# Two layers in one program: other dates, lanes and queues for the side work of the first two sequences

## The chip, the cores and the metric

The kernel runs on one core of a Trainium2 chip. The metric is the device time of one execution in microseconds. Before the change the median of three runs is 4860.24 us (4858.21 to 4866.17). All data are float32.

## The reference

Eight sequences of 1024 tokens with 256 features go through two layers. Cut to what matters:

```python
xn = layernorm(x)
x = x + causal_attention(xn) + routed_experts(xn)   # layer 0, 16 heads of 16
xn = layernorm(x)
x = x + attention(xn) + butterfly_ffn(xn)           # layer 1, 16 heads of 16
```

- `causal_attention` takes its softmax over the keys of a masked score matrix (masked entries are -10000, not minus infinity), so that the sum of later values enters with a small weight.
- `routed_experts` takes the softmax of 8 router logits, the best expert of each token, that expert's 256 x 256 matrix and bias, and multiplies by the gate.
- Layer 1's `attention` works on a log-mapped input `v`, its queries multiplied by a learned metric (two tanh layers); its output is multiplied by 0.1 and clipped.
- `butterfly_ffn` is a 256 to 1024 projection, ten butterfly stages, GELU, ten stages and a 1024 to 256 projection. The butterflies are linear, so they can be folded into the projections once for all tokens.

## The kernel before, in words

**Order.** Sixteen attentions follow one another: a0, a1, b0, a2, b1, a3 and so on (a is layer 0, b layer 1, the number the sequence). Each has four groups of heads, each group two halves of 512 queries, each half a number of *steps*, one for 128 keys: 4 and 8 for the causal layer, 8 and 8 for the other. So a0 is steps 1 to 48 and a1 steps 49 to 96. In a step TensorE computes the scores of two pairs of heads (L478), ScalarE takes the exponential (L485), for a block on the diagonal POOL clears what lies beyond it (`affine_select`, L487), and TensorE weighs the values (L503) one step later. Beside it runs a first pass for a later group: scores (L435), a mask added by VectorE where needed (L440) and row maxima (L444). The diagonal blocks of a0 are the four steps of each first half and the last four of each second half.

**Warm-up.** The first group's maxima have no scores to run beside. They are taken ahead of step 1 in twelve rounds of two maxima (the loop with `fill.step = -100`), with the step number at -99 to -88.

**Side work.** Everything else is written as generators, put as tasks into six lanes of a planner, `Fill`. A task has a cost (the TensorE time that it is thought to take, in ns; FULL is 855), a date `due`, a first step `after`, and a lead; its rank is `due - lead`. Only the head of a lane can run. After each step `spend` gives the tasks a budget, which follows from what is still to be done by each date (`rate`), and takes the ready task of lowest rank. A generator that yields `Rest` or `Later` cannot run again until so many steps have passed; tasks that last yielded `Rest` are moreover advanced, one piece every half step and at no cost, by `idle_engines`. `finish_due` runs all that is due at the start of a step to its end, one piece after another. The engines' queues are in order and the program's order is what this planner writes; each engine then waits on semaphores only.

**The tasks of the first sequence.** `gates0` computes values and router logits (per 128 tokens two matmuls and two VectorE additions, L614, L581, L619) and the best expert. `later0` makes suffix sums of the values: per tile one or two matmuls, and the running sum `rest` on POOL (L732, L734). `route0` ranks the tokens by expert (L657 to L698), scatters the normalized tokens into `sorted_d` in device memory with eight indirect DMAs issued by POOL (L703), two to a half step, and adds a bias to x on POOL (L570). `experts` handles 15 tiles of sorted tokens, each with a gather of the expert's matrix by POOL (L783), a load of the tokens by SP (L782), transposes (L806) and matmuls (L798), and a store to `mixed_d` by SP (L812). `collect` gathers the results (L829). `finish0` waits until a sequence is collected (`mixed`), transposes the attention's output (`outputs`) and projects it.

**The fold.** `multiply_paths` multiplies seven arrays of 128 x 2048, one after another, on POOL (L869). `fold` applies the products to the projections (`within`, L879, on TensorE), scales between blocks (`across`: ScalarE L893, VectorE L902 and L905, a copy by POOL L908), transposes (L947) and stores the folded weights. Layer 1 cannot begin without them.

The dates are set in `begin_attention` (L1209 on), where `s` holds the first steps of the four groups and the end: for a0 `s` is 0, 12, 24, 36, 48, and `starts[8]` is 96.

Of the kernel before, what the change touches and what calls it, by code (L numbers as in the profile page):

```python
# [12 lines left out]
ALU = mybir.AluOpType  # L13
# [9 lines left out]
DH = 1024  # L23
# [29 lines left out]


class Task:
    def __init__(self, gen, cost, due, after=0, lead=0):
        self.gen, self.cost, self.due, self.ready = gen, cost, due, after
        self.light = True
        self.rank = due - lead
# [142 lines left out]
def two_layers(ctx: ExitStack, tc: tile.TileContext, a: dict, out: bass.AP):  # L202
# [82 lines left out]
    paths = []  # L285
# [355 lines left out]
    def route0(att):  # L641

        b, n = att.b, att.n
        while b not in gates_of:
            yield Rest(0.5)
        yield Later(1)
        hot, gate = gates_of[b]
        shape = [P, NT, NE]

        rank = small.tile(shape, F32, tag="rank", name=f"rank_{n}", bufs=1)
        tot = small.tile(shape, F32, tag="tot", name=f"tot_{n}", bufs=1)
        of_e = small.tile([P, 3, NE], F32, tag="of_e", name=f"of_e_{n}", bufs=1)
# [12 lines left out]
        square = [P, NE, NE]  # L667
        sq = work.tile(square, F32, tag="es", name=f"sq_{n}", bufs=1)
        DVE.tensor_tensor(
            sq, tot[:, 0].unsqueeze(2).to_broadcast(square),  # L670
            tiles_from.unsqueeze(1).to_broadcast(square), ALU.is_gt,
        )
        DVE.tensor_reduce(num, sq, AX.X, ALU.add)
        DVE.tensor_tensor(sq, upto, num.unsqueeze(1).to_broadcast(square), ALU.mult)
        DVE.tensor_reduce(end, sq, AX.X, ALU.add)
        DVE.tensor_tensor(base, end, num, ALU.subtract)
        yield Rest(0.5)
        DVE.scalar_tensor_tensor(
            rank, base.unsqueeze(1).to_broadcast(shape), float(P), rank, ALU.mult, ALU.add
        )  # L680
        DVE.tensor_tensor(rank, rank, hot, ALU.mult)
        top = small.tile([P, NT], F32, tag="top", name=f"pos_{n}")
        DVE.tensor_reduce(top, rank, AX.X, ALU.add)
        slot_of = small.tile([P, NT], U32, tag="slot", name=f"slot_{n}")
        DVE.tensor_copy(slot_of, top)
        yield Rest(0.5)

        shape = [P, NS, NE]
        wide = work.tile(shape, F32, tag="es", name=f"wide_{n}", bufs=1)
        DVE.tensor_tensor(  # L690
            wide, end.unsqueeze(1).to_broadcast(shape), slot_no.unsqueeze(2).to_broadcast(shape),
            ALU.is_le,
        )
        ex = small.tile([P, NS], F32, tag="ex", name=f"ex_{n}", bufs=1)
        DVE.tensor_reduce(ex, wide, AX.X, ALU.add)
        DVE.tensor_scalar(ex, ex, float(NE - 1), float(P), ALU.min, ALU.mult)
        rows = small.tile([P, NS], U32, tag="rows", name=f"rows_{n}")
        DVE.tensor_scalar(rows, ex, row, None, ALU.add)  # L698
        yield Rest(0.5)
        xn, held = xn0.pop(b)  # L700
        yield from in_sorted.take()
        for t in range(NT):
            POOL.indirect_dma_start(  # L703
                sorted_d[:, :], bass.IndirectOffsetOnAxis(ap=slot_of[:, t : t + 1], axis=0),
                xn[:, t, :], None,
            )
            if t % 2:
                yield Rest(0.5)
        first.free(held)
        route_of[b] = slot_of, rows, gate  # L710
        yield from add_to_all(xs[b], outb)

    def later0(att):

        n = att.n
        while att.b not in gates_of:
            yield Rest(0.5)
        slot = None
        if att.b:
            slot = yield from second.take()  # L720
            later = work.tile([P, NT, D], F32, tag="second", name=f"later_{n}", bufs=1)
        else:
            later = work.tile([P, NT, D], F32, tag="h", name=f"later_{n}")
        att.slot = slot
        yield Later(0)
        rest = new = None
        for t in range(NT - 1, -1, -1):
            own = att.vals[:, t, :, 0:3:2, :]
            if t:
                new = small.tile([P, 8, 2, 16], F32, tag="rest", name=f"rest_{n}_{t}")  # L730
                if rest is None:
                    POOL.tensor_copy(new, own)  # L732
                else:
                    POOL.tensor_tensor(new, rest, own, ALU.add)  # L734
            ps = bank(f"later_{n}_{t}")
            PE.matmul(ps[:, :D], tri, own, start=True, stop=(rest is None))
            if rest is not None:
                PE.matmul(ps[:, :D], ones, rest, start=False, stop=True)
            ACT.copy(later[:, t, :], ps[:, :D])
            rest = new  # L740
            yield FULL
        att.later = later
# [98 lines left out]
    def finish0(att):  # L841
        b, n = att.b, att.n
        x = xs[b]
        while b not in mixed:
            yield Rest(0.5)
        sums = new_stats(f"b{b}")
        yield Later(0)
        for h in range(2):
            yield from att.outputs(h)
            for i in range(4):  # L850
                t = 4 * h + i
                ps = bank(f"y_{n}_{t}")
# [12 lines left out]

    def multiply_paths():

        for t in paths[1:]:
            POOL.tensor_tensor(paths[0], paths[0], t, ALU.mult)  # L869
            yield Rest(1)  # L870
        POOL.tensor_tensor(conb, conb, downb, ALU.add)
        folded.append("paths")

# [335 lines left out]
    def begin_attention(i):  # L1209
# [14 lines left out]
        if layer == 0 and b == 0:  # L1224
# [1 line left out]
            fill.add(0, later0(at[0, 0]), 8 * FULL, s[0] + 4)  # L1226
            fill.add(1, route0(at[0, 0]), 1, s[1])
            fill.add(1, prepare0(at[0, 1]), 4 * FULL, s[3])
            fill.add(1, gates0(at[0, 1]), 8 * FULL, s[4])
            fill.add(1, route0(at[0, 1]), 1, s[4])  # L1230
            fill.add(1, later0(at[0, 1]), 8 * FULL, s[4])
            fill.add(2, experts(0), 20 * FULL, s[4] - 8, 0, 24)
            fill.add(2, collect(0), 0, s[4])
            fill.add(2, experts(1), 20 * FULL, starts[8] - 10, 0, 24)
            fill.add(2, collect(1), 0, starts[8])
            fill.add(3, multiply_paths(), 0, s[1])
            fill.add(3, fold(), 12 * FULL, s[4] - 4)
        elif layer == 0 and b == 1:
            fill.add(0, prepare1(at[1, 0]), 8 * FULL, s[3])
            fill.add(0, values1(at[1, 0]), 8 * FULL, s[4])  # L1240
# [5 lines left out]
        else:  # L1246
            if b == 0:
                fill.add(1, prepare0(at[0, 2]), 4 * FULL, s[2], s[0] + 2)
            if b + 1 < NB:
                fill.add(0, prepare1(at[1, b + 1]), 8 * FULL, s[3], 0, 24)  # L1250
                fill.add(3, metric1(at[1, b + 1]), 32 * FULL, s[4] + 8 if b + 2 < NB else s[3])
            if b + 2 < NB:
                fill.add(1, gates0(at[0, b + 2]), 8 * FULL, s[1] + 4, s[0] + 2, 12)
                fill.add(1, route0(at[0, b + 2]), 1, s[2], 0, 20)
                fill.add(1, later0(at[0, b + 2]), 8 * FULL, s[4])
                fill.add(2, experts(b + 2), 20 * FULL, s[4] + 16, 0, 48)
                fill.add(4, collect(b + 2), 0, s[4] + 42)
            if b == NB - 2:
                fill.add(0, values1(at[1, b + 1]), 8 * FULL, s[4])
# [70 lines left out]
    while halves[0].i == 0:  # L1330
        first_pass(1)
        first_pass(0)
        fill.step += 1
        fill.now = fill.step
        fill.idle_engines()
        fill.spend(2 * FULL, 0.0)
        fill.release()
        put(now)
        now += 1
# [174 lines left out]
```

## Time and profile before

| | |
|---|---|
| median of three runs | 4860.24 us |
| the profiled execution | 4863.26 us |
| its span, first to last instruction | 4861.3 us |
| busy: PE / DVE / ACT / POOL | 4682.4 / 3070.2 / 2219.5 / 773.4 us |
| mean granted TensorE clock | 0.982 |
| DMA | 158.27 MB, 33 GB/s on average |

The page lists the busy time of each engine, the same in 40 slices of 121.5 us each (a digit is the busy share in tenths), and the costliest groups of instructions by line. A line of the form `L734 POOL TENSOR_TENSOR ...` is line 734 of the kernel; `x48` counts instructions. In the list of waits, `PE av_a L503 <- POOL p_a L487: 12.1, 1, 12.1` says that TensorE's matmul of line 503 waited for POOL's line 487, in total 12.1 us, once, the longest wait 12.1 us. The same questions can be put to a stretch of the span, given in us from its start. Names lose their numbers: `a0` and `a1` both show as `a`. PE is the matmul stream, PEld its weight loads.

### The profile page before, as it was taken

The page shows a single profiled execution, that of the slowest core. Times are in us where ns is not written, and L with a number is a line of the kernel's source. Part 1 is how long each engine was busy: PE and PEld are TensorE (multiplying, and loading weights), DVE is VectorE, ACT ScalarE, POOL GpSimd, SP SyncE. Part 2 cuts the span into 40 slices and gives each one's busy share as a digit, 9 for nine tenths or more (in the row PEclk, how much of TensorE's full clock was granted, in tenths as well). Part 3 has the DMA queues.
Part 4 walks back from the last instruction along what each step waited for, and adds up shares of the span by engine and source line. Part 5 has one row for each costly group of instructions (what it writes and reads, how often), then busy time and mean ns, then how long its engine had stood idle before and what let it go on. Part 6 is the DMA issues. An engine that isn't in the chain of part 4 may idle for free.

```text
span 4861.3 us, 69082 instructions
## 1 busy us (share of the span) xinstructions
PE 4682.4 (96%) x27808; PEld 1876.4 (39%) x27808; DVE 3070.2 (63%) x5010; ACT 2219.5 (46%) x2925; POOL 773.4 (16%) x1308
## 2 busy tenths in 40 slices
PE   7879999999999999999999999999999999999998
PEld 3334344344333443334443344334443344333332
DVE  5666665665666657666576666766667665666553
ACT  1343444544455444554345544455444544455544
POOL 3333300211120111201102111021211111110000
PEclk7989999999999999999999999999999999999999
DMA  3111200111001110012000110011100110000000
GB/s 136 61 59 59 71 2 16 33 54 40 12 18 33 55 36 3 23 39 68 15 1 28 40 62 15 1 39 40 54 13 10 34 55 27 20 1 10 1 9 9
DMA packets 85679, 158.27 MB, mean 33 GB/s; under 512 B 12657, under 2 KB 67569, under 8 KB 82161
## 3 DMA queue, kind: packets, MB, share of 16 engines
q1 hardware_dynamic: 69616, 89.88, 5.5%
q0 software_dynamic: 15744, 63.98, 4.0%
q8 instruction: 220, 3.60, 0.3%
q14 instruction: 99, 0.80, 0.1%
HBM read 117.25 MB, written 36.57 MB: 32 GB/s over the span
## 4 chain that ended last, share of the span: by engine, by line
PE 86%; DVE 6%; ACT 3%; issue 3%; POOL 1%; DMA 1%; POOLq 0%; DVEq 0%; SPq 0%; ACTq 0%
PE sc_b L478 18%; PE av_b L503 10%; PE sc_a L478 10%; PE mx_b L435 6%; PE av_a L503 5%; PE w L1149 5%; PE mx_a L435 5%; PE f L390 5%; PE h_b L390 3%; PE g_b L1076 2%; PE e L798 2%; ACT p_b L485 1%; PE q_b L390 1%; PE v_b L1036 1%; PE k_b L390 1%
## 5 line engine op out<-in xcount | busy, mean ns | idle before, releaser
L444 DVE TENSOR_REDUCE mm_b<-mx_b 128x2 f32<-128x1024 f32 x1024 | 1251.8, 1223 | 754.2 <-PE mx_b L435 753.5
L485 ACT ACTIVATE p_b<-sc_b 128x1024 f32<-128x1024 f32 x1024 | 1044.9, 1023 | 1092.2 <-PE mx_b L435 630.9
L435 PE MATMUL mx_b<-kT_b,qT_b 32*128 32x512 f32 x4096 | 1158.3, 642 | 10.9 <-ACT p_b L485 7.0
L478 PE MATMUL sc_b<-qT_b,kT_b 32*128 32x512 f32 x4096 | 1141.2, 638 | 7.9 <-ACT p_b L485 2.7
L485 ACT ACTIVATE p_a<-sc_a 128x1024 f32<-128x1024 f32 (+3 forms) x768 | 620.2, 809 | 905.2 <-PE sc_a L478 636.5
L444 DVE TENSOR_REDUCE mm_a<-mx_a 128x2 f32<-128x1024 f32 (+3 forms) x768 | 734.3, 957 | 219.7 <-PE mx_a L435 201.2
L435 PE MATMUL mx_a<-kT_a,qT_a 32*128 32x512 f32 (+3 forms) x3072 | 715.9, 549 | 15.4 <-DVE mm_a L444 6.6
L478 PE MATMUL sc_a<-qT_a,kT_a 32*128 32x512 f32 (+3 forms) x3072 | 713.3, 542 | 3.3 <-DVE mm_a L444 2.0
L503 PE MATMUL av_b<-p_b,vals 128*32 128x512 f32 x4096 | 554.1, 605 | 1.5 <-ACT p_b L485 1.5
L478 PEld LDWEIGHTS sc_b<-qT_b,kT_b 32*128 32x128 f32 x4096 | 305.9, 183 | 622.3 <-issue 402.1
L440 DVE TENSOR_TENSOR mx_a<-mx_a,cst 128x256 f32<-128x256 f32 x512 | 220.0, 430 | 389.4 <-PE sc_a L478 184.0
L487 POOL TENSOR_SCALAR_AFFINE_SELECT p_a<-p_a 128x256 f32<-128x256 f32 x512 | 209.6, 410 | 1355.7 <-ACT p_a L485 1337.2
L478 PEld LDWEIGHTS sc_a<-qT_a,kT_a 32*128 32x128 f32 x3072 | 234.5, 186 | 378.4 <-issue 273.0
L503 PE MATMUL av_a<-p_a,vals 128*32 128x512 f32 (+3 forms) x3072 | 337.6, 506 | 13.0 <-POOL p_a L487 13.0
L435 PEld LDWEIGHTS mx_b<-kT_b,qT_b 32*128 32x128 f32 x4096 | 307.1, 183 | 56.0 <-ACT p_b L485 42.2
L783 POOL DMA_INDIRECT ew<-in_ew,rows_a x120 | 116.6, 972 | 1081.9 <-PE mx_b L435 439.9
L1149 PE MATMUL w<-wcon,f 128*128 128x256 f32 x1024 | 276.5, 399 | 0.0
L435 PEld LDWEIGHTS mx_a<-kT_a,qT_a 32*128 32x128 f32 x3072 | 238.0, 188 | 70.5 <-ACT p_a L485 34.7
L1149 PEld LDWEIGHTS w<-wcon,f 128*128 128x128 f32 x1024 | 179.6, 191 | 141.7 <-issue 119.2
L503 PEld LDWEIGHTS av_b<-p_b,vals 128*32 128x32 f32 x4096 | 81.7, 108 | 391.5 <-issue 382.6
L390 PE MATMUL f<-xT_b,wexp 128*128 128x512 f32 x512 | 223.9, 595 | 0.0
L503 PEld LDWEIGHTS av_a<-p_a,vals 128*32 128x32 f32 x3072 | 62.3, 109 | 277.6 <-issue 208.7
(211 smaller groups left out, 4214.9 us busy)
## 6 DMA issues: line engine op xcount, KB each, us to landing
ew<-sorted_d SPq DMA_DIRECT2D x120, 128.0 KB, 3.1
mixed_d<-ew SPq DMA_DIRECT2D x120, 128.0 KB, 1.7
x<-in_x SPq DMA_DIRECT2D x8, 1024.0 KB, 5.6
wexp<-wexp_d SPq DMA_DIRECT2D x8, 1024.0 KB, 6.5
wcon<-wcon_d SPq DMA_DIRECT2D x8, 1024.0 KB, 6.3
out<-x SPq DMA_DIRECT2D x8, 1024.0 KB, 9.2
paths<-in_paths SPq DMA_DIRECT2D x7, 1024.0 KB, 12.5
w<-in_w1t SPq DMA_DIRECT2D x8, 512.0 KB, 3.8
```

Source lines behind the costliest of these rows:

```text
L390: PE.matmul(ps, w[:, c, cols : cols + P], rhs[:, c, h * 512 : (h + 1) * 512], start=(c == 0), stop=(c == 1),)
L435: PE.matmul(sc[:, j, :w], qT[r : r + 32, t * P : (t + 1) * P], kT[r : r + 32, k * 512 : k * 512 + w], start=True, stop=True,)
L440: DVE.tensor_tensor(sc[:, :, w - P : w], sc[:, :, w - P : w], negmask.unsqueeze(1).to_broadcast([P, 2, P]), ALU.add,)
L444: DVE.tensor_reduce(mm[:, t, 2 * pr : 2 * pr + 2, k], sc[:, :, :w], AX.X, ALU.max)
L478: PE.matmul(sc[:, j, c0:], kT[r : r + 32, kt * P : (kt + 1) * P], qT[r : r + 32, h * 512 + c0 : (h + 1) * 512], start=True, stop=True,)
L485: ACT.activation(p[:, :, c0:], sc[:, :, c0:], AF.Exp, scale=0.25)
L487: POOL.affine_select(p[:, :, c0 : c0 + P], p[:, :, c0 : c0 + P], [[0, 2], [1, P]], ALU.is_ge, 0.0, base=0, channel_multiplier=-1,)
L503: PE.matmul(av[32 * i : 32 * i + 32, c0:], self.vals[:, kt, 4 * (g // 2) + i, odd : odd + 2, :].rearrange("p e d -> p (e d)"), p2[i // 2][ ...
L783: POOL.indirect_dma_start(halves[:, s % 2, : 3 * D], None, a["ew"], bass.IndirectOffsetOnAxis(ap=rows[:, s : s + 1], axis=0),)
L798: PE.matmul(ps[:, :D], was[:, c * P : (c + 1) * P], w[:, c * D : (c + 1) * D], start=(c == 0), stop=(c == 1),)
L1076: PE.matmul(ps, w2t[:, m, c * P : (c + 1) * P], hT[:, m, :], start=(m == 0), stop=(m == 3),)
L1149: PE.matmul(ps[:, :D], hT[k // 4][:, k % 4, i * P : (i + 1) * P], wcon[:, k, :], start=(k == 0), stop=(k == 7),)
```

## The change

- A task's default `after` is minus infinity, not 0, so tasks without a date of their own are ready in the warm-up. Those that had 0 written out now have `s[0]`, or `s[0] - 99` for `experts(0)` and `fold`.
- In each round of the warm-up the idle engines are served twice, at the round's number and half a step later.
- `multiply_paths` multiplies halves of 1024 columns and rests half a step after each.
- `route0` rests half a step after each scatter, not after every second one.
- `later0` keeps its running sum on VectorE for sequence 0 (`on`), on POOL for the others.
- `finish0` runs `outputs` of a half before it waits for `mixed`.
- Dates, leads and lanes of sequences 0 and 1 differ, as below. `later0` of a1 moves from lane 1 to lane 0.

```diff
-    def __init__(self, gen, cost, due, after=0, lead=0):
+    def __init__(self, gen, cost, due, after=-math.inf, lead=0):
...
                 xn[:, t, :], None,
             )
-            if t % 2:
-                yield Rest(0.5)
+            yield Rest(0.5)
...
+                on = POOL if att.b else DVE
                 if rest is None:
-                    POOL.tensor_copy(new, own)
+                    on.tensor_copy(new, own)
                 else:
-                    POOL.tensor_tensor(new, rest, own, ALU.add)
+                    on.tensor_tensor(new, rest, own, ALU.add)
...
         x = xs[b]
-        while b not in mixed:
-            yield Rest(0.5)
         sums = new_stats(f"b{b}")
         yield Later(0)
         for h in range(2):
             yield from att.outputs(h)
+            while b not in mixed:
+                yield Later(0.5)
...
         for t in paths[1:]:
-            POOL.tensor_tensor(paths[0], paths[0], t, ALU.mult)
-            yield Rest(1)
+            for i in range(2):
+                part = slice(i * DH, (i + 1) * DH)
+                POOL.tensor_tensor(paths[0][:, part], paths[0][:, part], t[:, part], ALU.mult)
+                yield Rest(0.5)
...
             fill.add(1, prepare0(at[0, 1]), 4 * FULL, s[3])
-            fill.add(1, gates0(at[0, 1]), 8 * FULL, s[4])
-            fill.add(1, route0(at[0, 1]), 1, s[4])
-            fill.add(1, later0(at[0, 1]), 8 * FULL, s[4])
-            fill.add(2, experts(0), 20 * FULL, s[4] - 8, 0, 24)
-            fill.add(2, collect(0), 0, s[4])
-            fill.add(2, experts(1), 20 * FULL, starts[8] - 10, 0, 24)
+            fill.add(1, gates0(at[0, 1]), 8 * FULL, s[4], s[0], 40)
+            fill.add(1, route0(at[0, 1]), 1, s[4], s[0], 40)
+            fill.add(0, later0(at[0, 1]), 8 * FULL, s[4])
+            fill.add(2, experts(0), 20 * FULL, s[4] - 4, s[0] - 99, 44)
+            fill.add(2, collect(0), 0, s[4] + 4)
+            fill.add(2, experts(1), 20 * FULL, starts[8] - 10, s[0], 24)
             fill.add(2, collect(1), 0, starts[8])
             fill.add(3, multiply_paths(), 0, s[1])
-            fill.add(3, fold(), 12 * FULL, s[4] - 4)
+            fill.add(3, fold(), 12 * FULL, s[4] + 4, s[0] - 99, 30)
...
         fill.step += 1
-        fill.now = fill.step
-        fill.idle_engines()
+        for fill.now in (fill.step, fill.step + 0.5):
+            fill.idle_engines()
         fill.spend(2 * FULL, 0.0)
```

For the later sequences three tasks (`prepare1`, `route0`, `experts`) have `s[0]` in place of 0 as their first step.

More of the change, by code (lines that the diff above doesn't have):

```diff
@@ L1249, in begin_attention @@
             if b + 1 < NB:
-                fill.add(0, prepare1(at[1, b + 1]), 8 * FULL, s[3], 0, 24)
+                fill.add(0, prepare1(at[1, b + 1]), 8 * FULL, s[3], s[0], 24)
                 fill.add(3, metric1(at[1, b + 1]), 32 * FULL, s[4] + 8 if b + 2 < NB else s[3])
@@ L1253, in begin_attention @@
                 fill.add(1, gates0(at[0, b + 2]), 8 * FULL, s[1] + 4, s[0] + 2, 12)
-                fill.add(1, route0(at[0, b + 2]), 1, s[2], 0, 20)
+                fill.add(1, route0(at[0, b + 2]), 1, s[2], s[0], 20)
                 fill.add(1, later0(at[0, b + 2]), 8 * FULL, s[4])
-                fill.add(2, experts(b + 2), 20 * FULL, s[4] + 16, 0, 48)
+                fill.add(2, experts(b + 2), 20 * FULL, s[4] + 16, s[0], 48)
                 fill.add(4, collect(b + 2), 0, s[4] + 42)
```

## The prediction

> **What bounds the kernel now.** First the page, busy shares and slices:
>
> ```profile
> PE 4682.4 (96%) x27808; PEld 1876.4 (39%) x27808; DVE 3070.2 (63%) x5010; ACT 2219.5 (46%) x2925; POOL 773.4 (16%) x1308
> ...
> PE   7879999999999999999999999999999999999998
> ...
> POOL 3333300211120111201102111021211111110000
> PEclk7989999999999999999999999999999999999999
> ```
>
> TensorE fills the span; its 179 us of idleness lie almost wholly in the first three slices, where POOL is busiest and the granted clock below full. So I cut the start into stages and asked for the busy time of each. Cuts: first maximum matmul (25.2), first value matmul of a0 (57.4), first score matmul (67.9), and the score matmuls after that, eight records to a step: steps 1 to 12 end at 169.0, 13 to 36 at 287.9, 37 to 48 (the end of a0) at 395.0. Columns: window, its length, busy time of PE, PEld, DVE, ACT, POOL, clock, DMA share, GB/s.
>
> ```profile
> 25.20:57.40 32.20, 26.91 (x101) 11.59 (x101) 29.90 (x48) 2.06 (x4) 0.00 (x0) 0.56 0.64 214
> 57.40:67.90 10.50, 10.48 (x36) 8.44 (x36) 4.34 (x16) 0.00 (x1) 0.00 (x0) 0.72 0.00 0
> 67.90:169.00 101.10, 68.81 (x356) 26.93 (x355) 49.51 (x99) 24.83 (x39) 59.88 (x67) 0.75 0.13 44
> 169.00:287.90 118.90, 115.25 (x755) 52.23 (x751) 89.86 (x189) 56.30 (x91) 30.59 (x64) 0.99 0.18 61
> 287.90:395.00 107.10, 73.36 (x390) 32.09 (x390) 60.35 (x130) 39.84 (x71) 45.86 (x82) 0.79 0.20 68
> ```
>
> Steps 13 to 36 show what this stretch can do: PE idle 3.6 of 118.9 us, full clock. The two stages of twelve steps beside it lose 32 and 34 us to idleness and more to the halved clock; in the warm-up (first row) VectorE is full (29.9 of 32.2) and POOL does nothing. What ended the idle time, 67.9 to 395, in the waits of PE:
>
> ```profile
> PE wx L947 <- POOL wx L908: 19.4, 4, 17.1
> PE av_a L503 <- POOL p_a L487: 12.1, 1, 12.1
> PE later_a L738 <- POOL rest_a L734: 7.4, 3, 3.6
> PE later_a L738 <- POOL rest_a L732: 5.8, 2, 4.0
> PE e L806 <- DMA ew<-sorted_d: 4.5, 1, 4.5
> ```
>
> All are chains through POOL or a transfer. The groups of POOL and DVE in steps 1 to 12 say which:
>
> ```profile
> L869 POOL TENSOR_TENSOR paths<-paths,paths 128x2048 f32<-128x2048 f32 x6 | 27.0, 4508 | 0.0
> L703 POOL DMA_INDIRECT sorted_d<-xn_a,slot_a x8 | 8.0, 995 | 14.7 <-DMA sorted_d<-xn_a,slot_a 13.3 <-DVE slot_a L685 1.4
> ...
> L669 DVE TENSOR_TENSOR sq_a<-tot_a,cst 128x64 f32<-128x64 f32 x1 | 3.7, 3715 | 0.0
> L551 DVE TENSOR_TENSOR on_a<-es_a,rc_a 128x256 f32<-128x256 f32 x1 | 3.6, 3560 | 0.0
> ```
>
> Six path products of 4.5 us stand in POOL's queue ahead of masks (L487) and suffix sums (L734); eight scatters hold it for 22.7 us, as each waits for the one before to land; and L669 and L551, some 0.23 and 0.42 us elsewhere, end with a product.
>
> **The change, part by part.** The sum is made against the profiled execution: 4863.3 us (span 4861.3 and 2.0 around it), 3.0 over the median.
>
> What a step costs. Fill in steps 13 to 36 by spacing in the chain: 11 expert tiles at 1.06 with 11 transposes at 0.38 (15.8), 8 value tiles at 0.99 (7.9), four projections at 1.96 (7.8), 16 transposes (2.0), four path matmul groups at 1.06 (4.2), the bias (1.7): 39.4. (118.9 - 39.4) / 24 = 3.3 us a step, twelve steps 40.
>
> *Warm-up, 32.2 us.* Now no task is ready before step 0, for the default date is 0 and the warm-up counts from -99; value tiles run alone afterwards (10.5 us). With the new default twelve rounds offer 1.7 us of fill each. By the ranks: rounds 1 to 4 the eight value tiles, 5 and 6 the gate's small operations, 7 to 10 the eight suffix-sum tiles, 11 and 12 the ranks' matmuls and the first four path groups. VectorE pays: 8 x (0.425 + 0.156) = 4.6, ten small operations at 0.2 (2.1), seven suffix sums moved from POOL to DVE at 0.42 (L551's usual duration; 3.0), routing's 11 at 0.2 (2.3): 12. The path products start on an idle POOL as soon as the paths have landed (their 8 KB packets arrive from 20.3 to 41.1 us) and take 27 us, until about 52. Until then a DVE operation with two SBUF inputs can wait for a half product, 4.5 / 2: the gate's four and two sums, six of them, 0 to 13.5 us; I take half a wait each, 6. VectorE's 2.3 us of idleness fill up. 32.2 + 12 + 6 - 2.3 = 48, so step 1 starts near 73; bounds 67 (no collision) and 90 (TensorE kept at half clock: 26.9 and twice the 19 us of added matmuls, 65). The polls in half steps and conb's add (0.74) lie on the idle POOL; the two weight loads of the fold go past SP, which has nothing else by then.
>
> The row for collisions is L669. [...] The clock row reads 0.56 with PE busy 26.9 of 32.2. [...]
>
> *Steps 1 to 12, 101.1 us.* Gone: products, suffix sums, path groups. Left: 40, the bias 1.7 and three expert tiles (3.3). Routing's first scatter moves from step 8 to step 1, two a step to step 5, each 2.7 us of POOL (they start at 135.16, 137.85, 140.51) with two masks at 0.41: 6.2 us a step. Queued behind them are the masks of steps 1 to 4, all diagonal; the weighing of every step waits for those. 4 x (6.2 - 3.3) = 11.6; bounds 0 (the weighing lags a step) and 22.7. The fold's scaling moves here from steps 23 on: per step two ACT (0.50), two DVE (0.48) and a POOL copy (0.40) that waits for DVE, at 2.4 us a time in the old place (28.9 / 12), where PE was hardly idle; nothing, or 10 if masks queue behind it. I take 4 with the clock. Sum 61.
>
> *Steps 13 to 36, 118.9.* Experts come first (rank 0), one tile every second step because of the waits between them; path groups and transposes share the others, so value tiles of a1 come later, five rather than eight. Three fewer, 3.0, and nothing else: 115 (bounds 110, 125). On SP the store of the first folded weight now stands among the experts' loads; it waits for one ScalarE copy (L883, 0.59), and a tile has two steps until it is needed: 0 to 1.
>
> *Steps 37 to 48, 107.1.* Gone is what is forced at its date: three expert tiles at step 40 (the 4.5 us wait) and the fold at 44 (19.4). Fill: projections 7.8, two expert tiles 2.9, three value tiles 3.0, transposes 3.4, suffix sums 6.4, ranks 0.5: 24. With 40: 64. By the ranks a1's gates end near step 43 and its scatters start near 47, so up to seven are forced at 48: 7 x 2.7 and eight adds at 0.73, 25 us of POOL ahead of a mask, less the 7 us a weighing can lag. Bounds 0 (scatters done by then) and 25; I take 12, between a paced and a forced row. Small waits 5. Sum 81.
>
> *After.* Turning outputs ahead of the wait costs nothing: the transposes (two groups of 0.5) run beside the last gather. But collect(0) now ends at 52, not 48, so finish0's projections come three steps later: 0 to 15, taken 5, for prepare1 starts later while rates go by dates. For sequences 2 to 7 mixed is set long before, and dates of s[0] for 0 change nothing. Single scatters there are spread; 0, at most 5 either way.
>
> End of step 48: 73 + 61 + 115 + 81 = 330 for 395, gain 65, less 5: 60. 4863.3 - 60 = 4803, in a median execution 4800. From 600 on PE is busy for 4182.6 of 4261 us at full clock, so that all of it moves forward unchanged.
>
> **Rivals.**
> 1. The warm-up becomes the bound: half clock, step 1 at 90, and the diagonal scatters cost 22.7, not 11.6. 28 less: 4828. For it: the clock 0.56; against: PE busy is mostly VectorE's back-pressure.
> 2. The forced stretch only moves: step 48 takes the full 25, and the waits of 37 to 48 stay otherwise (107). 26 less: 4826. For it: serial routing cannot be shortened; against: the fold, 19.4, has no date there.
> 3. Slower: experts(1) starts only after collect(0), at 52, and needs 16 tiles by step 86. A tile forced there costs the wait for its rows, 4.5 us (L806). With 15 or more forced, 68 us, the gain is gone: 4868, and 4872 with 16. It decides if experts(1) has hardly begun by 84. Against it: before, it took one tile a step from 63 to 73.
> 4. The change doesn't act: the fill in the warm-up just lengthens it by what it saves, and the forced chains stay: 4850 to 4870.
>
> **How the numbers follow.** Forecast 0.63 (own range 4775 to 4822), rival 1 0.13, rival 2 0.13, rival 3 0.06, rival 4 0.05. The sum's best ends (67, 45, 110, 64, nothing after) reach 4751, its worst (90, 78, 125, 94, 15) 4867. 8 in 10 with both milder rivals: 4763 to 4846. A measurement tells 0.2% (10 us) from nothing, so the line is 4850: faster 0.87, same 0.05, slower 0.08 (rival 3 and part of 4).
>
> **What would show it.** Products before 55 us; value and suffix-sum tiles between maxima; step 1 at 67 to 90; no wait of L947 on L908 over 2 us; the largest wait left that of L503 on masks behind scatters, in steps 1 to 5 and at 48. I am wrong if step 1 comes later still, or a stage after 395 loses more than 15 us.

## The result

| | before | after |
|---|---|---|
| median (range) of 15 runs each | 4860.14 us (4856.98 to 4866.40) | 4873.91 us (4865.84 to 4878.96) |
| span of the profiled execution | 4861.3 us | 4874.8 us |
| mean granted clock | 0.982 | 0.982 |

The changed kernel is a little slower: ratio 1.0026, 95% interval 1.0018 to 1.0034. The forecast was 4800, with 8 in 100 for slower. The page of the changed kernel shows almost nothing of it: busy times and slices are those of before to a tenth here and there.

```profile
PE 4683.3 (96%) x27808; PEld 1871.3 (38%) x27808; DVE 3081.6 (63%) x5017; ACT 2215.7 (45%) x2925; POOL 773.7 (16%) x1307
...
PE   7889999999999999999999999999999999999998
...
POOL 4232201111020110211102111111111111110000
PEclk7989999999999999999999999999999999999999
```

TensorE's busy time grew by 0.9 us only; the other 12.6 of the 13.5 us of span are idle time (178.9 before, 191.5 after). Where it lies is seen when both spans are cut at the same *steps*. The exponential of each step (L485) is a mark that both kernels have; this table, worked out from the starts of these 1792 instructions, has the start of some steps in us and how much later the changed kernel reaches them.

| step | before | after | after minus before |
|---|---|---|---|
| 1 (a0 begins) | 69.5 | 82.1 | +12.6 |
| 13 | 168.6 | 155.3 | -13.3 |
| 37 | 287.6 | 272.6 | -15.1 |
| 49 (a1) | 394.8 | 349.8 | -45.0 |
| 61 | 462.0 | 432.4 | -29.6 |
| 97 (b0) | 677.6 | 652.5 | -25.2 |
| 209 (b1) | 1297.9 | 1272.7 | -25.2 |
| 321 (b2) | 1881.7 | 1863.1 | -18.6 |
| 433 (b3) | 2467.4 | 2453.5 | -13.9 |
| 545 (b4) | 3048.2 | 3043.7 | -4.5 |
| 657 (b5) | 3632.2 | 3636.7 | +4.5 |
| 769 (b6) | 4209.4 | 4223.4 | +14.0 |
| end | 4861.3 | 4874.8 | +13.5 |

So the first two sequences did get faster, by 25 us and not 60, and five later stretches gave back 39. In these the two programs differ in little but the rest after each scatter; the experiments below undo that alone. In the trace the two kernels look like this, cut at steps 209 and 769 among others: window, length, TensorE's busy time, clock. First after:

```profile
349.80:652.40 302.60, 274.94 (x1578) 0.94 0.14 46
652.40:1272.70 620.30, 608.72 (x3620) 1.00 0.09 30
1272.70:4223.40 2950.70, 2877.85 (x17332) 0.99 0.09 30
4223.40:4874.80 651.40, 623.69 (x3640) 0.99 0.02 7
```

and before:

```profile
394.80:677.60 282.80, 270.97 (x1581) 0.98 0.14 46
677.60:1297.90 620.30, 608.73 (x3620) 1.00 0.09 30
1297.90:4209.40 2911.50, 2872.82 (x17332) 1.00 0.09 30
4209.40:4861.30 651.90, 623.90 (x3640) 0.99 0.02 7
```

The third row is the loss: the same 17332 matmuls in 2950.7 instead of 2911.5 us, with 34 us more idleness and 5 us more of busy time at a clock a little lower. The second and fourth rows are equal within 0.5 us. No digit of the 40 slices shows it, since it is 1.3% of a stretch that reads 9 everywhere.

What TensorE waits for in that third stretch of the changed kernel:

```profile
PE e L806 <- DMA ew<-sorted_d: 20.5, 5, 4.2
PE nm_a L468 <- ACT p_a L485: 7.3, 5, 1.5
PE v_b L1038 <- DVE vals L578: 6.0, 5, 1.2
```

Each comes five times, once in each stretch of 112 steps; before, the longest total there was 5.5 us, and L806 was not among the waits that the list begins with. The second of the five, at step 399, in the timeline of TensorE:

```profile
2259.04 1.03 PE L798 MATMUL e<-ew,et 128*128 128x256 f32 x4
2259.90 0.38 PE L806 MATMUL e<-cst,ew 128*128 128x128 f32 x2
2260.80 1.13 PE L798 MATMUL e<-ew,et 128*128 128x256 f32 x4 [0.52 <-DVE et L809]
2266.12 0.69 PE L806 MATMUL e<-cst,ew 128*128 128x128 f32 x2 [4.20 <-DMA ew<-sorted_d]
2267.33 2.08 PE L798 MATMUL e<-ew,et 128*128 128x256 f32 x4 [0.52 <-DVE et L809]
```

and in windows (length, then busy time of PE, PEld, DVE, ACT, POOL, the clock, DMA share, GB/s):

```profile
2257.00:2261.00 4.00, 3.28 (x15) 2.68 (x16) 2.01 (x6) 0.00 (x0) 0.00 (x0) 1.00 0.00 0
2261.00:2265.00 4.00, 0.93 (x4) 0.47 (x3) 0.07 (x1) 0.00 (x0) 1.00 (x1) 0.94 0.41 134
2265.00:2270.20 5.20, 3.56 (x18) 2.11 (x22) 1.18 (x3) 0.00 (x0) 0.00 (x0) 0.50 0.14 50
```

Three expert tiles stand there in a row, forced by their date; before it was one. The last cannot fetch its matrix and rows until the buffer of an earlier one is free: its gather waits for the matmuls of that one,

```profile
POOL ew L783 <- PE e L798: 5.7, 1, 5.7
```

and so TensorE waits 4.2 us, and then works 5 us at half clock: the same four matmuls of L798 take 2.08 and not 1.03 us. The step takes 17.3 us; before it took 3.6.

The stages of the first two sequences in the changed kernel, cut at the first score matmul (80.0) and then at steps 13, 37, 49 and 61, same columns:

```profile
25.20:80.00 54.80, 42.81 (x188) 23.89 (x184) 42.61 (x84) 6.95 (x17) 21.52 (x23) 0.81 0.50 163
80.00:155.30 75.30, 61.28 (x331) 24.48 (x334) 54.38 (x119) 29.33 (x51) 30.98 (x51) 0.70 0.14 46
155.30:272.60 117.30, 112.96 (x730) 48.38 (x724) 86.38 (x181) 57.73 (x92) 31.41 (x65) 0.96 0.21 68
272.60:349.80 77.20, 69.54 (x392) 28.98 (x384) 47.39 (x103) 28.41 (x45) 25.62 (x52) 0.91 0.16 53
349.80:432.40 82.60, 59.90 (x394) 27.56 (x394) 50.56 (x106) 22.48 (x31) 25.85 (x43) 0.88 0.15 47
```

And the waits of TensorE from 67.9 to 395 us, the window whose waits were shown of before:

```profile
PE av_a L503 <- POOL p_a L487: 15.8, 2, 14.9
PE nm_a L468 <- ACT e_a L461: 7.7, 2, 5.1
PE sc_a L478 <- DVE mm_a L444: 3.4, 4, 2.2
PE later_a L738 <- POOL rest_a L734: 3.1, 2, 2.2
```

The fold's wait (L947 on L908, 19.4 us) is gone, that for the suffix sums on POOL (13.2 us) has shrunk to 5.8, and the largest one left is a mask behind scatters, at the beginning of a1. POOL there, in the changed kernel:

```profile
348.95 0.96 POOL L703 DMA_INDIRECT sorted_d<-xn_a,slot_a  x1 [1.95 <-DMA sorted_d<-xn_a,slot_a]
351.89 0.96 POOL L703 DMA_INDIRECT sorted_d<-xn_a,slot_a  x1 [1.97 <-DMA sorted_d<-xn_a,slot_a]
354.80 0.97 POOL L703 DMA_INDIRECT sorted_d<-xn_a,slot_a  x1 [1.95 <-DMA sorted_d<-xn_a,slot_a]
357.71 0.96 POOL L703 DMA_INDIRECT sorted_d<-xn_a,slot_a  x1 [1.94 <-DMA sorted_d<-xn_a,slot_a]
358.69 5.47 POOL L570 TENSOR_TENSOR x<-x,outb 128x256 f32<-128x256 f32 x8
364.12 0.40 POOL L487 TENSOR_SCALAR_AFFINE_SELECT p_a<-p_a 128x256 f32<-128x256 f32 x1
```

Four forced scatters, each of which waits until the one before has landed, and eight additions of 0.68 us keep the mask waiting until 364.1.

### The profile page after: what moved, and what is told of

It is laid out like the page before. It is cut to its first block, busy times and chain, and to the rows that moved or that the text cites. A ratio compares the mean times of both kernels' runs of the same rounds, so it can differ in the third digit from the quotient of the medians.

```text
span 4874.8 us, 69112 instructions
## 1 busy us (share of the span) xinstructions
PE 4683.3 (96%) x27808; PEld 1871.3 (38%) x27808; DVE 3081.6 (63%) x5017; ACT 2215.7 (45%) x2925; POOL 773.7 (16%) x1307
## 4 chain that ended last, share of the span: by engine, by line
PE 88%; DVE 6%; ACT 3%; DMA 1%; issue 1%; POOL 1%; POOLq 0%; DVEq 0%; SPq 0%; ACTq 0%
PE sc_b L478 18%; PE av_b L503 10%; PE sc_a L478 10%; PE mx_b L435 6%; PE av_a L503 6%; PE w L1151 5%; PE mx_a L435 5%; PE f L390 5%; PE h_b L390 3%; PE g_b L1078 3%; PE e L798 2%; DVE mm_a L444 1%; ACT p_b L485 1%; PE q_a L390 1%; PE k_a L390 1%; PE q_b L390 1%
## 5 line engine op out<-in xcount | busy, mean ns | idle before, releaser
L485 ACT ACTIVATE p_b<-sc_b 128x1024 f32<-128x1024 f32 x1024 | 1044.9, 1023 | 1105.1 <-PE mx_b L435 619.0
L435 PE MATMUL mx_b<-kT_b,qT_b 32*128 32x512 f32 x4096 | 1155.9, 640 | 10.6 <-ACT p_b L485 6.8
L485 ACT ACTIVATE p_a<-sc_a 128x1024 f32<-128x1024 f32 (+3 forms) x768 | 619.9, 809 | 918.2 <-PE sc_a L478 633.8
L503 PE MATMUL av_b<-p_b,vals 128*32 128x512 f32 x4096 | 554.1, 605 | 1.5 <-ACT p_b L485 1.5
L487 POOL TENSOR_SCALAR_AFFINE_SELECT p_a<-p_a 128x256 f32<-128x256 f32 x512 | 209.8, 412 | 1393.3 <-ACT p_a L485 1363.5
L503 PE MATMUL av_a<-p_a,vals 128*32 128x512 f32 (+3 forms) x3072 | 343.4, 512 | 15.8 <-POOL p_a L487 15.8
L783 POOL DMA_INDIRECT ew<-in_ew,rows_a x120 | 117.0, 975 | 911.3 <-PE mx_b L435 429.3
L503 PEld LDWEIGHTS av_b<-p_b,vals 128*32 128x32 f32 x4096 | 81.7, 108 | 392.2 <-issue 383.3
L503 PEld LDWEIGHTS av_a<-p_a,vals 128*32 128x32 f32 x3072 | 62.8, 109 | 283.1 <-issue 210.5
## 6 DMA issues: line engine op xcount, KB each, us to landing
paths<-in_paths SPq DMA_DIRECT2D x7, 1024.0 KB, 12.6
```

Source lines behind the costliest of these rows:

```text
L435: PE.matmul(sc[:, j, :w], qT[r : r + 32, t * P : (t + 1) * P], kT[r : r + 32, k * 512 : k * 512 + w], start=True, stop=True,)
L485: ACT.activation(p[:, :, c0:], sc[:, :, c0:], AF.Exp, scale=0.25)
L487: POOL.affine_select(p[:, :, c0 : c0 + P], p[:, :, c0 : c0 + P], [[0, 2], [1, P]], ALU.is_ge, 0.0, base=0, channel_multiplier=-1,)
L503: PE.matmul(av[32 * i : 32 * i + 32, c0:], self.vals[:, kt, 4 * (g // 2) + i, odd : odd + 2, :].rearrange("p e d -> p (e d)"), p2[i // 2][ ...
L783: POOL.indirect_dma_start(halves[:, s % 2, : 3 * D], None, a["ew"], bass.IndirectOffsetOnAxis(ap=rows[:, s : s + 1], axis=0),)
```

## The experiments

Twelve kernels in three sets, each timed beside the kernel before (medians 4860.4, 4863.1 and 4861.5). Letters of theories are those of the quoted texts; A and B blame the single scatters, A because they make the expert tiles late for their date, B because of the scatters themselves; C is any other part of the change. E and P, further down, are A and B again, for lateness and for the scatters themselves (E in the text for route_date is another rival). Executions of one and the same program differ by some us in the first twelve steps: six of these kernels and the changed one are the same up to step 40 at least, and they reach step 13 at 149.9 to 155.3. So differences under 6 us are read with care, and across the sets all the more, as the kernel before itself differs by 2.7 us between them.

### Are the single scatters of the later sequences the loss? (pairs_later, singles_alone)

Pairs again for sequences 2 to 7, all else as changed:

```diff
-            yield Rest(0.5)
+            if b < 2 or t % 2:
+                yield Rest(0.5)
```

> The changed kernel, with single scatters kept for sequences 0 and 1 alone; from sequence 2 on route0 scatters two to a half step, as before the change. Theory A: in the trace of the changed kernel the gain stands at 25.2 us up to step 209 and is lost in five portions (a3 to a7), 38.7 us in all, where two more expert tiles are forced at their date because the slower scatters let experts begin later. Then this kernel takes 4874 - 39 = 4835 us (4829 to 4842) and its steps 287, 399, 511, 623 and 735 are as short as before the change. Theory B: the single scatters themselves stand in the way on POOL; the same 4835. Theory C: the turned outputs or the dates of the later sequences cost it: 4874 as it is.

4828.74 us (4822.26 to 4829.56), ratio to before 0.9936 (0.9919 to 0.9953). And the kernel before with nothing but the single scatters, in all sequences:

```diff
-            if t % 2:
-                yield Rest(0.5)
+            yield Rest(0.5)
```

> The kernel before, with one edit alone: route0 rests half a step after every scatter. Theories A and B: the later sequences lose 39 us, so 4860 + 39 = 4899, and up to 20 more in the first two sequences, where the dates before the change then force expert tiles at step 40 and a1's routing at step 48: 4895 to 4920. Theory C: 4860, at most 5 either way.

4904.17 us (4901.35 to 4905.22), ratio 1.0089 (1.0072 to 1.0106). One line, undone alone, turns the change from 14 us slower into 32 faster; done alone, it costs 44. From step 297 to step 645 singles_alone runs parallel to the changed kernel: it is 30.4 to 31.5 us behind it at every step, so that nothing but this line is at work there. C falls. The same stretch of pairs_later:

```profile
1265.80:4168.60 2902.80, 2864.28 (x17332) 1.00 0.10 30
```

It is 47.9 us shorter than in the changed kernel. It is also 8.7 us shorter than before, with the same work there. That is the clock, not the order: 7.7 us of it lie in steps 312, 424, 425 and 623, over which the granted clock reads 0.73, 0.70, 0.68 and 0.80 before and 1.00 in pairs_later, while the waits in steps 424 and 425 are the same (0.7 and 0.3 us). The profiled execution is moreover the fastest of this kernel's four (4822.26 us). Why the clock falls there in the one execution and not in the other was not followed.

### The date of the expert tiles (experts_date)

In the changed kernel, `experts(b+2)` due eight steps later, same rank:

```diff
-                fill.add(2, experts(b + 2), 20 * FULL, s[4] + 16, s[0], 48)
+                fill.add(2, experts(b + 2), 20 * FULL, s[4] + 24, s[0], 56)
```

> The changed kernel with single scatters everywhere, but the experts of sequences 2 to 7 due 8 steps later (s[4] + 24, with the lead raised by 8, so that the rank stays). Nothing of the scatters changes. Theory A, forced tiles: none is forced any more, 4874 - 39 = 4835 or up to 10 lower, since the one tile forced in the kernel before goes too. Theory B, the scatters' own time on POOL: 4874. Theory C: 4874.

4874.79 us (4869.98 to 4879.87), ratio 1.0032 (1.0019 to 1.0044): not one us better, though the burst is gone. Step 287 takes 2.9 us, not 17.1, and L806 is no longer among the first waits. But step 321 to step 433 takes 590.5 us, as in the changed kernel (590.4; pairs_later 580.6). Against pairs_later it now loses 4.8 us in steps 352 and 353, where the rest of a4's routing is forced beside more of `prepare1` than in the changed kernel, and 5.7 in steps 426 and 430, where `collect` and the butterflies end later than they did. Steps 352 and 353 in windows (columns as above):

```profile
2017.90:2027.70 9.80, 7.00 (x42) 1.98 (x36) 7.58 (x14) 4.82 (x5) 9.35 (x10) 0.98 0.29 80
2027.70:2035.10 7.40, 6.31 (x22) 2.42 (x26) 3.19 (x7) 2.44 (x5) 0.00 (x0) 0.56 0.01 2
```

POOL is full (9.35 of 9.80), TensorE lacks 2.8 us, and the clock after it reads 0.56. So A in its narrow form, that this one date is to blame, falls here: late work that is spared at one date is forced at another.

### Lateness or the scatters? (late_experts, gates_early)

Two kernels part the two. In the first the scatters are in pairs, but the experts may not start before step `s[0] + 33`, about as late as in the changed kernel:

```diff
 (pairs_later)
-                fill.add(2, experts(b + 2), 20 * FULL, s[4] + 16, s[0], 48)
+                fill.add(2, experts(b + 2), 20 * FULL, s[4] + 16, s[0] + 33, 48)
```

> Pairs of scatters in the later sequences (4828.7 with that alone), and experts(b+2) not ready before s[0] + 33, so that its first tiles and those left for its date stand as in the changed kernel although the scatters do not. Theory E, that single scatters cost what they cost only by making the experts late: five cycles at 9 us more, 4874 (4865 to 4880). Theory P, that the scatters themselves, POOL's queue and the masks behind them are what costs: 4829 (4824 to 4834).

4907.05 us (4907.05 to 4908.15), ratio 1.0091 (1.0074 to 1.0108). No scatter differs from pairs_later, and the loss is there, larger than forecast: 11 to 21 us in each of the five stretches. The experts are in fact later than in the changed kernel: the first matmuls of a4's tiles come at step 365, not 362 (356 in pairs_later), and four tiles stand at step 399, not three. Its waits from 1275 to 4255 us begin with the same line, with twice the count:

```profile
PE e L807 <- DMA ew<-sorted_d: 25.8, 10, 4.5
```

In the second the scatters stay single, but routing starts sooner, since the gates before it are due sooner:

```diff
 (the changed kernel)
-                fill.add(1, gates0(at[0, b + 2]), 8 * FULL, s[1] + 4, s[0] + 2, 12)
+                fill.add(1, gates0(at[0, b + 2]), 8 * FULL, s[1] - 1, s[0] + 2, 12)
```

> The changed kernel with its single scatters in all sequences, and only gates0(b+2) due at s[1] - 1, not s[1] + 4: by the planner's order routing then begins ten steps sooner, the expert tiles too, and none but the last store is left for the date. Theory E: the loss of the later cycles goes, 4830 (4824 to 4838), if the gates cost no more where they now stand. Theory P: eight single scatters are still there, 4874 (4866 to 4880).

4843.56 us (4841.01 to 4847.88), ratio 0.9958 (0.9941 to 0.9975): 30 of the 45 us between the changed kernel and pairs_later are back, with every single scatter in place. What is missing to 4829 lies elsewhere: against pairs_later each of the stretches loses 5.0 to 5.7 us in its first sixteen steps, where `finish0` now stands closer together ahead of the routing, and most win some 2 back. At step 399 it loses nothing: a4's first tile comes at step 350, and none is left for the date.

So E holds: lateness costs without single scatters, and single scatters without lateness cost little. Why they make the experts late is in the code and in part in the trace. A resting task gets its turn each half step only while no unit of side work is left open across the step (`advance` serves the idle engines only if `holder` is None). By the planner's order that is so in every step of steps 1 to 5, and in every second step where `metric1` runs beside the routing, so eight scatters take eight turns there and not four. (This is read from the code and was not tested by itself.) In the trace the eight start from 1975.0 to 2016.3 us in the changed kernel, in 41.3 us, against 1958.3 to 1980.0, 21.7 us, in pairs_later. The first six keep the same pace in both, some 16 us; the last two come late, since they now stand in POOL's queue behind operations of `prepare1` (L963), the first of which waits 13 us for VectorE:

```profile
2005.31 1.68 POOL L963 TENSOR_TENSOR y0r_b<-y_b,half 128x8 f32<-128x8 f32 x1 [12.99 <-DVE y_b L976]
2007.18 1.03 POOL L703 DMA_INDIRECT sorted_d<-xn_a,slot_a  x1 [0.20 <-issue]
```

The experts' first gather (L783) follows at step 352, not 348, and the tiles, some three steps from one to the next, all follow. It is the place in the order that counts: in experts_date all eight scatters have started by 1995.7 us, and the first gather still comes at 2017.8, behind the first of the same operations of `prepare1`.

### The routing of a1 at step 48 (route_date)

pairs_later with `route0(a1)` due six steps later, at the same rank:

```diff
-            fill.add(1, route0(at[0, 1]), 1, s[4], s[0], 40)
+            fill.add(1, route0(at[0, 1]), 1, s[4] + 6, s[0], 46)
```

> As pairs_later, and route0 of a1 due 6 steps later (s[4] + 6, lead 46, same rank), so that its last five scatters and eight adds are not forced at step 48 but go on in half steps to step 52. Theory D: the 14.9 us in which TensorE waits there for a mask behind them are lost to this date; 4835 - 15 = 4820 (4815 to 4826), and no wait of L503 on L487 over 4 us near step 48. Rival E: POOL needs the time anyway and the masks of steps 49 to 52, all diagonal, wait instead, each a little: 4835.

4817.83 us (4814.23 to 4818.56), ratio 0.9911 (0.9894 to 0.9927), the fastest of all. Step 49 takes 6.4 us, not 20.4; steps 50 to 60 give 4 back. TensorE's waits from 340 to 432 us, which in pairs_later begin with 14.2 us of L503 on the mask:

```profile
PE e L807 <- DMA ew<-sorted_d: 3.2, 2, 2.8
PE later_a L739 <- POOL rest_a L735: 3.0, 1, 3.0
```

Here nothing else is pushed on: the experts of a1 wait for `collect(0)` anyway, and their tiles stand at steps 57 to 74 as in pairs_later and before, so the scatters can end later without making them late.

### The parts of the first two sequences

All on top of pairs_later (4828.7), each with one part undone; then two that go on from these. Tasks ready from step 0 on, not in the warm-up (`no_warm`):

```diff
-    def __init__(self, gen, cost, due, after=-math.inf, lead=0):
+    def __init__(self, gen, cost, due, after=0, lead=0):
...
-            fill.add(2, experts(0), 20 * FULL, s[4] - 4, s[0] - 99, 44)
+            fill.add(2, experts(0), 20 * FULL, s[4] - 4, s[0], 44)
...
-            fill.add(3, fold(), 12 * FULL, s[4] + 4, s[0] - 99, 30)
+            fill.add(3, fold(), 12 * FULL, s[4] + 4, s[0], 30)
```

> Pairs in the later sequences (4828.7), and tasks ready as before, from step 0 on: nothing but the halves, lanes, dates and leads of the first two sequences is left of the change. Theory W, that readiness in the warm-up is what gains in steps 1 to 12: step 1 at 70, not 79, but step 13 near 169, not 150, and by the planner's order the fold and four scatters are forced at 48 and 52: 19 more, and up to 10 for those, 4848 to 4858. Theory L, that the warm-up only pays for itself and dates and lanes bring the gain: 4829 (4822 to 4836).

4836.82 us (4835.53 to 4839.60), ratio 0.9947 (0.9931 to 0.9964): 8 us more than pairs_later (5 when each is taken against before in its own set), at the upper end of what L gives. Step 1 starts at 68.6, not 78.9, and step 13 at 145.7, even before that of pairs_later (149.9); it falls behind after that, by 5 us up to step 37 and by 8 in steps 49 to 60, where the fold ends, at step 51 and not 43 (61 is reached at 439.4, against 429.4). So readiness in the warm-up moves work ahead of step 1 for about what it lengthens the warm-up by, and pays by what comes later.

The running sum of sequence 0 back on POOL, in no_warm (`no_warm_pool`):

```diff
-                on = POOL if att.b else DVE
+                on = POOL
```

> As no_warm (4836.8), and the running sum of sequence 0 back on POOL, behind the path products. If the move to VectorE is what took away TensorE's waits for L732 and L734, 11.0 us in steps 1 to 12 of the kernel before: 4848 (4844 to 4853). If halves of the products alone are enough for the sums to come between them: 4838 (4835 to 4841).

4845.18 us (4839.46 to 4846.34), ratio 0.9960 (0.9946 to 0.9974): 8 us more than no_warm, and step 13 is reached 12.0 us later, of which 9 remain at step 49. Its waits from 67 to 400 us begin with

```profile
PE later_a L739 <- POOL rest_a L735: 16.3, 5, 4.3
PE av_a L503 <- POOL p_a L487: 11.9, 6, 7.6
```

so the halves alone don't let the sums through; moving the sums to VectorE does.

Whole products (`full_products`):

```diff
-            for i in range(2):
-                part = slice(i * DH, (i + 1) * DH)
-                POOL.tensor_tensor(paths[0][:, part], paths[0][:, part], t[:, part], ALU.mult)
-                yield Rest(0.5)
+            POOL.tensor_tensor(paths[0], paths[0], t, ALU.mult)
+            yield Rest(0.5)
```

> Pairs in the later sequences (4828.7), and whole path products of 4.5 us, not halves of 2.3. If VectorE's small operations in the warm-up wait for the product that they meet, as the 1.9 and 2.3 us of L457 and L460 in the changed kernel say, three such waits get 2.2 us longer each: 4835 (4832 to 4840). If the halves serve nothing: 4829 (4825 to 4832).

4830.94 us (4828.12 to 4832.44), ratio 0.9932 (0.9915 to 0.9949). The first step starts at 82.9 us in the profiled execution, 4.0 later than in pairs_later, but the executions with halves have it at 78.9 to 82.2, and the times do not differ by more than they spread: nearer to halves that serve nothing, a few us at most.

Pairs in all sequences (`pairs_all`, `if t % 2:`):

> Scatters in pairs in all sequences, the rest of the change in place; pairs in the later sequences alone gave 4828.7. If single scatters serve the first two sequences, each of the pairs of steps 1 to 5 holds a mask for one scatter of 2.7 us more: 4836 (4832 to 4842). If a weighing can lag by that much: 4829 (4824 to 4832).

4832.87 us (4829.17 to 4833.94), ratio 0.9938 (0.9921 to 0.9954). Step 13 comes at 157.3, later than in any of the seven executions with single scatters there, but the time is 4 us more at most; between the two expectations, and not settled.

`finish0` waiting before its first outputs, as before (`wait_first`):

```diff
+        while b not in mixed:
+            yield Rest(0.5)
...
-            while b not in mixed:
-                yield Later(0.5)
```

> Pairs in the later sequences (4828.7), and finish0 waits for the collected rows before it turns the first outputs, as in the kernel before. If turning ahead of the wait costs and brings nothing, as the forecast has it: 4829 (4825 to 4833). If it is worth the step by which finish0(a0) now ends sooner in the planner's order: 4834.

4826.61 us (4821.31 to 4833.05), ratio 0.9924 (0.9907 to 0.9940): no difference.

Only the path products ready in the warm-up, with the date of route_date (`paths_warm_route`, no_warm with this):

```diff
-            fill.add(3, multiply_paths(), 0, s[1])
+            fill.add(3, multiply_paths(), 0, s[1], s[0] - 99)
...
-            fill.add(1, route0(at[0, 1]), 1, s[4], s[0], 40)
+            fill.add(1, route0(at[0, 1]), 1, s[4] + 6, s[0], 46)
```

> Of all tasks only the path products are ready in the warm-up, the rest from step 0 on; pairs in the later sequences; a1's routing due six steps later, which gave 4817.8 with all tasks ready. If it is VectorE's added operations that lengthen the warm-up: step 1 near 70 and not 79, steps 1 to 12 six us longer, and the single forced steps at 44 and 52 a few us: 4818 (4812 to 4824). If the products alone lengthen it: step 1 at 75 or later, 4825 (4822 to 4832).

4828.13 us (4825.46 to 4836.24), ratio 0.9929 (0.9912 to 0.9945): 10 more than route_date. Step 1 starts at 73.9, between the two expectations: in these executions the products alone lengthen the warm-up by some 5 us and VectorE's additions by another 5. Step 13 is reached 8.8 us sooner than in route_date; steps 13 to 24 lose 6.8, 37 to 60 lose 12. In those the routing and the fold of a0 stand later, and `collect(0)` is forced at 52. That what is late there is what costs, as in experts_date, was not tested apart.

## Why the prediction was wrong

**The step that failed** is one sentence on the later sequences: "Single scatters there are spread; 0, at most 5 either way." Measured: 39 us over five stretches against before, 48 against pairs_later. It took the pace of the first two sequences (one scatter each half step) for that of all, and did not ask who waits for the last scatter: the experts, which have a date. The forecast did name the warning sign, "a stage after 395 loses more than 15 us", and its rival 3 had the mechanism, tiles forced at their date for a wait of 4.5 us each (4.2 measured), but looked for it at step 86 of a1, where nothing of it is seen, and asked for 15 tiles. Two more a stretch are enough: the three of step 399 make it 17.3 us instead of 3.6, with 4.2 us of waiting and half clock after it, and what is late at one date pushes other work on.

**The sum for the first two sequences** had 60 and 25.2 was measured. Term by term, against the stage lengths of both kernels (steps 37 to 60 taken together, for a1's forced scatters hold the mask of step 49, not 48):

| term | forecast | measured | of which missing |
|---|---|---|---|
| step 1 begins | +5.1 (first score matmul at 73) | +12.6 (first exponential; the first score matmul, at 80.0, +12.1) | 7.5 |
| steps 1 to 12 | -40.1 (61) | -25.9 (99.1 to 73.2) | 14.2 |
| steps 13 to 36 | -3.9 (115) | -1.7 (119.0 to 117.3) | 2.2 |
| steps 37 to 60 | -26.1 | -14.6 (174.4 to 159.8) | 11.5 |
| after | +5.0 | +4.4 (steps 61 to 209) | -0.6 |
| sum | -60.0 | -25.2 | 34.8 |

- *Warm-up.* The products start at 15.79 and last till 43.5, twelve halves of 2.3 us, and not until about 52. The forecast had misread when the paths land: its 20.3 to 41.1 us count from the first DMA record, 10.3 us ahead of the span; in the span's time the packets arrive from 10.0 to 30.8. Three small operations of VectorE show the collision: L457 1.91 us (0.17 elsewhere), L460 2.27 (0.18), L462 0.76 (0.18). That is 4.4 us, and 6 were taken. The added operations were sized rightly too. What fell is that VectorE would be full: it is busy for 42.6 of the 54.8 us, while TensorE waits 12 us in all for the last logits (4.9, L619), the running sums (3.0, L734), L460 (2.2) and some small ones. The chain goes to and fro between the two engines and left each idle for 12 us here, so the sum of one engine's busy time was no upper bound. That TensorE would not stay at the 0.56 that its clock read in this stage before was the author's estimate; in the changed kernel it averaged 0.81 from 25.2 to 80.0 us.
- *Steps 1 to 12.* The scatters took no more than was said: they start 2.7 to 4.6 us apart from 86.4 us on, steps 2 and 3 take 5.0 us each, where 6.2 was forecast, and no wait of L503 on L487 is in the list of TensorE's waits from 80 to 155 us. So the 11.6 us for masks behind scatters were nothing as a wait; what was too small is the 3.3 us a step, an average over steps 13 to 36 at full clock. Here the clock read 0.50 until 116 us. Over the twelve steps it averaged 0.70, less than before (0.75), with TensorE idle for 14.0 us and not 32.3. And steps 4 and 12 take 10.3 and 10.6 us, as before (10.1 and 9.8): the last operations of a half group in a row (L468 waits 7.7 us for L461), which the average spread out. The clock is not all of it: in route_date, the same program up to there, it averaged 0.82, and the stage still took 71.3 us, with 17.2 idle. Rival 1 (half clock at the start) was nearer for this stage, but put the price on the warm-up and on the masks.
- *Steps 13 to 36* ended within the bounds.
- *The end of a0.* By the forecast, up to seven scatters are forced and a weighing lags 7 us of it; 12 was taken. Five were forced, the last four of them seen above from 348.9 on, and TensorE waited 14.9 us for the mask; step 49 took 22.1 us against 4.9 before, 17 more. So 5 of the 11.5 missing lie there; the rest was not followed. The fold's wait of 19.4 us went as forecast. route_date confirms the size: 14.0 us off that step.
- *After.* "Turning outputs ahead of the wait costs nothing" holds (wait_first). For the three steps' delay of `finish0` 5 was taken, and 4.4 are lost after step 61; that this delay is the cause was not tested.
- "From 600 on ... all of it moves forward unchanged" was right for the two stretches that the scatters don't touch, 652 to 1273 and the last 651 us.

Rival 4 (no effect) would have been 4850 to 4870; the measured time is just above it for another reason.

## What to carry to other kernels

A change of pace was not free here, where the task has successors with dates: find the last instruction of the task, count who starts after it, and follow that chain to its date, in every stage that runs the line and not only in the one that it was changed for. The date moved at the end of such a chain only moved the loss (experts_date); the chain's earlier start brought most of it back (gates_early). Where nothing waited for the late work, moving its date paid (route_date). And cut both spans at marks that both kernels share before reading anything: a loss of 1.3% spread over five stretches is in no slice, and a list of waits for the whole span buries it.

## What was not expected of the hardware

The clock stayed halved through busy stretches. In the changed kernel TensorE is busy for nearly all of 80 to 92 us and of 96 to 104 in the records, and the granted clock reads 0.50 and stays there until 116 (columns: window, length, TensorE's busy time, clock, DMA share, GB/s):

```profile
76.00:80.00 4.00, 1.80 (x12) 1.00 0.00 0
80.00:84.00 4.00, 3.73 (x17) 0.50 0.01 4
84.00:88.00 4.00, 4.00 (x22) 0.50 0.00 0
88.00:92.00 4.00, 4.00 (x22) 0.50 0.09 33
96.00:100.00 4.00, 4.00 (x24) 0.50 0.18 66
100.00:104.00 4.00, 3.95 (x20) 0.50 0.09 33
```

In pairs_later, the same program up to there, it was back in the window 88 to 92 (0.70, then 1.00), and step 13 came 5.4 us sooner. A busy record does not tell how much a matmul does: 3.57 us of the window 84 to 88 are sixteen matmuls of one column each (L924). But the same sixteen run in pairs_later too, from 82.0 us on, ahead of the clock's return, so they alone are not the reason; it stays open. Nor do the rows give a length of idleness that goes with the halved clock: the 4.2 us wait at step 399 was followed by 0.50, but so were 2.2 us of work missing in the window 76 to 80.

The other surprise is how small an operation can collide. In the timelines of VectorE and POOL of the changed kernel:

```profile
39.34 1.91 DVE L457 TENSOR_TENSOR mxc_a<-mxc_a,cst 128x16 f32<-128x16 f32 x1
41.28 2.27 DVE L460 TENSOR_SCALAR negmax<-mxc_a 128x16 f32<-128x16 f32 x1
43.45 0.76 DVE L462 TENSOR_SCALAR e_a<-e_a 128x16 f32<-128x16 f32 x1
36.57 6.93 POOL L871 TENSOR_TENSOR paths<-paths,paths 128x1024 f32<-128x1024 f32 x3
43.47 0.72 POOL L873 TENSOR_TENSOR conb<-conb,downb 128x256 f32<-128x256 f32 x1
```

L460 has one input in SBUF, and 16 elements of each partition; it takes as long as a half product (2.3 us) and ends with one, like L457, which has two inputs; L462 ends with the addition of L873. The forecast counted operations with two inputs only in its sum.
